# A two-layer graph network: part of layer 2's matrix products issued in layer 1, with one PSUM store for both layers

## The chip, the cores and the metric

The kernel runs on one core of one Trainium2 chip. The metric is the device time of the whole kernel in microseconds (us). Before the change it is 1557.31 us, the median of 9 runs (1549.85 to 1561.43).

A core has five engines that each run their own list of instructions in order: PE (matmuls; PEld are its weight loads), DVE (vector work), ACT (activations and copies), POOL (here: issuing gathers) and SP (here: issuing most transfers). They wait for each other by semaphores. ACT issues the writes of layer 1's result.

## The reference

```python
src, dst = edge_index                        # 100000 edges, sorted by dst; 6250 nodes
def _gin_agg(h, src, dst, eps, n_nodes):
    agg = jax.ops.segment_sum(h[src], dst, num_segments=n_nodes)
    return (1.0 + eps) * h + agg
h = _gin_agg(x, src, dst, eps1, n)           # x: 6250 x 256
h = jax.nn.relu(h @ W1a + b1a)               # 256 -> 512
h = jax.nn.relu(h @ W1b + b1b)               # 512 -> 512: the result h1 of layer 1
h = _gin_agg(h, src, dst, eps2, n)           # 512 wide
h = jax.nn.relu(h @ W2a + b2a)               # 512 -> 512
out = h @ W2b + b2b                          # 512 -> 256
x = _layernorm(x + out, axis=-1)
```

The destinations are drawn as 6250 u^2 with u uniform, so low nodes have many edges and high nodes few. All is float32.

## The kernel before

**Tiles.** Nodes stand in 49 tiles of 128 rows (the last has 106). Edges stand in 782 chunks of 128. Tiles 0 to 4 (`HEAVY`) are the heavy ones. Their edges, 240 chunks, are not gathered: layer 1 counts them into a table of how often each source appears for each heavy destination, and each layer multiplies this table with its input. The other 542 chunks are gathered, once in each layer.

**Gathered chunks.** `gather` (L255) issues one indirect transfer on POOL for each chunk, 128 rows of the layer's input: 128 KB in layer 1 and 256 KB in layer 2. Chunks go in pieces of four (`BURST`), and six pieces may be under way (`PIECES`), so 24 gathers. The seventh piece's first gather waits for the sums of the first piece. In layer 1 the pieces lie in `early`, in layer 2 in `early` and `late`. The sums (L992) are matmuls of a 0/1 selection (`sel`, made on DVE in `select`, L598) with the gathered rows; a group of such sums is copied by ACT (L1011, `split`), turned to its tile rows by one more matmul (L1023, with `to`, L603), called a union here, and added on DVE into the sums of each tile that it reaches (L1015, `acc`).

**Accumulators.** `seed` (L566) loads the layer's input for a block of two tiles (`TILES`) into a buffer `acc` (SP, L577; the last tile L583) and has ACT scale it by 1 + eps (L584). There are `ACCS` = 8 such buffers, and `held` lists the blocks that have one.

**Counting and products.** In layer 1 `counting` (L804) builds the table in `at`, an SBUF tile of 49 x 522 16-bit numbers per partition, and `convert` (L857) turns it part by part to float32, into `cf`, and writes it to `counts` in DRAM (SP, L860). A part is one heavy tile by one range of four tiles of sources (`RANGE`); there are 13 ranges and 5 heavy tiles, so 65 parts. `products` (L744) takes part by part: `xr` holds the range's input rows (SP, L757), `cf` the part of the table, and the product is 4 matmuls (L784; one for the last range). In layer 1 a heavy tile's 13 products share one sum in PSUM. In layer 2 the table is read back (L799), each product is a PSUM bank of 512 columns of its own, and DVE adds it into `acc` (L790). A turn's transfers are issued one turn ahead.

**Blocks.** When all edges of a block of two tiles are in, `block` (L678) transposes its sums (L704), multiplies by the first weights (L720) and the second (L734); `finish1` writes h1's rows (L1046, L1048, ACT's transfer L1049), `finish2` and `conclude2` add x, normalise and write the result (L1071 to L1088).

**Order.** All is written out by a planner in the kernel's Python. The main loop goes over the groups of gathered chunks; after each chunk it calls `tick`, which does what was put off by `later` (taking PSUM results waits `LAG` = 7 ticks), and lets two queues issue work: `blockwise` (blocks, two at a time) and `beside` (counting or products). `spread` sets the rate of `beside` so that PE's estimated work per chunk is level; the late chunks carry most of the blocks, so the products lie in the earlier ones. After the last chunk a loop drains both queues.

**The seam.** Layer 2's first gather may read any row of h1, so it waits until all are written. In layer 2, POOL first issues 24 gathers; PE's list begins with five products, and then the sums. Layer 2 has its own SBUF pools (`edge2`, `dense2`, with `xr` and `cf`) and its own PSUM pool, in the room that layer 1's pools leave.

Of the kernel before, what the change touches and what calls it, by code (L numbers as in the profile page):

```python
# [24 lines left out]
W = 10  # L25
# [4 lines left out]
AHEAD = 4  # L30
ACCS = 8
LAG = 7
# [107 lines left out]
def tile_gin_residual_layernorm(  # L140
# [354 lines left out]
    def rows(t):  # L495
        return min(P, N - t * P)
# [18 lines left out]
    def ordered(ctx):  # L515
# [17 lines left out]
        counts = odram.tile([len(ranges), HEAVY, P, RANGE * P], F32, name="counts")  # L533

        def layer(number, ctx, table, width, scale, wa, ba, wb, wide, prepare, finish, conclude):
            kk = width // P
            edge = ctx.enter_context(tc.tile_pool(name=f"edge{number}", bufs=3))
            dense = ctx.enter_context(tc.tile_pool(name=f"dense{number}", bufs=2))
            psum = ctx.enter_context(
                tc.tile_pool(name=f"psum{number}", bufs=1, space=bass.MemoryType.PSUM)  # L540
            )
            banks = [
                psum.tile([P, BANK], F32, tag=f"bank{i}", name=f"bank{i}") for i in range(BANKS)
            ]
            halves = [(i, j) for i in range(BANKS) for j in range(2)]
            acc = {}
            held = []
            places = [early]
            if number == 2:
                late = edge.tile([P, PIECES * BURST * D], F32, name="late", bufs=1)  # L550
                places.append(late)
            sels = {}
            once = number == 1
            left = {
                t: (0 if t >= HEAVY else 1 if once else len(ranges)) for t in range(NT)
            }
            uses = {t: 0 for t in range(NT)}
# [7 lines left out]

            def seed(ts):  # L566
                while len(held) >= ACCS:
                    if not blockwise.todo:
                        due(all=True)
                    assert blockwise.todo  # L570
                    blockwise.step()
                    tick()
                held.append(ts)
                a = edge.tile([P, TILES, width], F32, tag="acc", name="acc", bufs=ACCS)
                n = whole(ts)
                if n:
                    nc.sync.dma_start(  # L577
                        a[:, :n, :],
                        table[ts[0] * P : (ts[0] + n) * P, :].rearrange("(k p) d -> p k d", p=P),
                    )  # L580
                if n < len(ts):
                    nc.vector.memset(a[:, n, :], 0.0)
                    nc.sync.dma_start(a[: rows(ts[n]), n, :], table[ts[n] * P : N, :])  # L583
                later(5, lambda: nc.scalar.activation(  # L584
                    a[:, : len(ts), :], a[:, : len(ts), :], AF.Copy, scale=scale
                ))
                for i, t in enumerate(ts):
                    acc[t] = a[:, i, :]

            def select(g):  # L590
                c0, h = groups[g]
                n = min(PARTS * h, NCH - c0)
                small = h == 1
                sel = edge.tile(
                    [P, PARTS if small else GRP, SLOTS], F32, name="sel",
                    tag="sel1" if small else "sel", bufs=4 if small else 2,
                )
                nc.vector.tensor_tensor(  # L598
                    sel[:, :n, :], iota[:, :SLOTS].unsqueeze(1).to_broadcast([P, n, SLOTS]),
                    slot[:, c0 : c0 + n].unsqueeze(2).to_broadcast([P, n, SLOTS]), op=ALU.is_equal,  # L600
                )
                to = edge.tile([P, P], F32, tag="to", name="to", bufs=6)
                nc.vector.tensor_scalar(to, iota, home[:, g : g + 1], None, op0=ALU.is_equal)  # L603
                sels[g] = sel, to

            delayed = []
            now = 0

            def later(chunks, what, frees=False):
                delayed.append((now + chunks, what, frees))

            def undelay(item):
                delayed.remove(item)
                item[1]()

            def due(all=False):
                while delayed:
                    item = min(delayed, key=lambda d: d[0])  # L620
                    if not all and item[0] > now:
                        break
                    undelay(item)
                for b in list(waiting):
# [4 lines left out]
            def tick():  # L629
                nonlocal now  # L630
                now += 1
                due()

            opened = []

            def place(n, whole=False):

                while True:
                    here = [h for h in halves if h[0] not in opened]
                    single = [h for h in here if (h[0], 1 - h[1]) not in halves]
                    double = [h for h in here if (h[0], 1 - h[1]) in halves]
                    if 2 * n <= BANK and (single or double):
                        i, j = (single or double)[0]
                        mine = [(i, j)]
                        break
                    if 2 * n > BANK and double:

                        i = next(h[0] for k, h in enumerate(double) if (h[0], 1 - h[1]) in double[:k])
                        j = 0
                        mine = [(i, 0), (i, 1)]
                        break
                    undelay(min((d for d in delayed if d[2]), key=lambda d: d[0]))
                for h in mine:
                    halves.remove(h)
                if not whole:
                    opened.append(i)
                return banks[i][:, j * BANK // 2 : j * BANK // 2 + n], mine  # L660

            def complete(p):
                opened.remove(p[1][0][0])

            def free(p):
                halves.extend(p[1])

            def take_later(p, what):

                def take():  # L670
                    what(p[0])
                    free(p)

                later(LAG, take, frees=True)

            def block(ts):  # L678
# [20 lines left out]
                for i, t in enumerate(ts):  # L699
# [10 lines left out]
                    ))  # L710
                    if t == ts[-1]:
                        held.remove(ts)
# [31 lines left out]
            def products(turns, table_of):  # L744
# [28 lines left out]
                for i, (r, t) in enumerate(turns):  # L773
# [3 lines left out]
                    ks = ranges[r]  # L777
                    opens = not once or r == 0
                    closes = not once or r == len(ranges) - 1
                    if opens:  # L780
# [16 lines left out]

            def load_counts(cf, r, ks, t):
                nc.sync.dma_start(  # L799
                    cf[:, : len(ks), :].rearrange("p k j -> p (k j)"),  # L800
                    counts[r, t, :, : len(ks) * P],
                )

            def counting():  # L804

                assert HEAVY <= 2 * RING
                room = RING * P + W
                at = edge.tile([P, NT, room], mybir.dt.uint16, tag="at", name="at", bufs=1)  # L810
                F16 = mybir.dt.float16
# [139 lines left out]
            if number == 2:  # L951
                for i in range(PIECES):
                    gathered[i] = gather(i, table, width, *places)
            for b in blocks:
                if b[0] < HEAVY:
                    seed(b)
            due(all=True)
            select(order[0])
            select(order[1])
            blockwise = Queue(4.0, BLOCKS)  # L960
            work = 0.00167 * HEAVY * NT * width
            if number == 1:
                work += 8.0 + STEP * NC + ADD * len(STEPS)
                aside = counting()
            else:
                aside = products([(r, t) for r in range(len(ranges)) for t in heavy],
                                     load_counts)
            rates = spread(
                groups, N, E, PACES[number - 1] * work, 0.00167 * KH * (width + wide)
            )  # L970
            beside = Queue(rates[0])
            beside.todo.append(aside)
            if number == 2:
# [4 lines left out]
            for k, g in enumerate(order):  # L978
# [10 lines left out]
                while upto < len(pieces) and pieces[upto][0] == g:  # L989
# [11 lines left out]
                    for c, b in pieces[upto][1]:  # L1001
                        tick()
                        for q in both:
                            q.pump()
# [27 lines left out]
                if k + 2 < len(order):  # L1032
                    n = len(members[order[k + 1]])
                    later(n // 2 if n > PARTS else 0, lambda k=k: select(order[k + 2]))
            while any(q.todo for q in both) or waiting:
                for q in both:
                    q.step()
                    tick()
# [5 lines left out]
        def finish1(dense, t, m, po, i, early):  # L1044
# [3 lines left out]
            nc.scalar.activation(h[:m], y[:m], AF.Relu)  # L1048
            nc.scalar.dma_start(h1[t * P : t * P + m, :], h[:m])  # L1049

        def conclude1(dense, ts, early):
# [25 lines left out]
        def conclude2(dense, ts, early):  # L1077
# [17 lines left out]
            if n:  # L1095
# [3 lines left out]
                )  # L1099

        with ExitStack() as inner:
            layer(1, inner, x, D, e1[:, 0:1], w1a_s, b1a_s, w1b_s, H, prepare1, finish1, conclude1)
# [254 lines left out]
```

## Time and profile before

The profiled execution took 1555.25 us; the span of its records is 1553.5 us.

| What | us | Where from |
|---|---|---|
| median of 9 runs | 1557.31 | the times |
| the profiled execution, and the span in it | 1555.25, 1553.5 | the times |
| PE busy in the span | 1368.8 (88%) | page, part 1 |
| POOL busy in the span | 1044.8 (67%) | page, part 1 |
| DVE, ACT busy | 707.9 (46%), 390.8 (25%) | page, part 1 |
| 542 gathers of layer 1, mean of one | 0.973 | page, part 5 |
| L784, 980 records | 361.3 busy | page, part 5 |
| last gather of layer 1 starts | 701.29 | POOL in order of time |
| first and last gather of layer 2 start | 766.13, 1452.01 | POOL in order of time |
| last sum of layer 2 starts | 1472.36 | PE in order of time |

Layer 1 runs from about 40 to 766 and layer 2 from there to the end. A PE row counts records, of which a float32 matmul leaves two, so "x8" at L784 is one product. Their ends are modelled; the distance of the starts is the sounder number. Rows with "<-" name what ended the idle time before them. A granted clock (PEclk) of 1.00 is full speed.

### The profile page before, as it was taken

Reading aid. Unit: us, or ns where it says so; the run is one execution under the profiler, and the core shown is the slowest. Engines: PE = TensorE matmul, PEld = TensorE weight load, DVE = VectorE, ACT = ScalarE, POOL = GpSimd, SP = SyncE. Lnnn points to the kernel's source line nnn. Section 1 sums busy time; section 2 is a strip of 40 time slices with the busy share of each in tenths; the row PEclk is TensorE's granted clock in tenths of the full one; section 3 lists DMA queues with packets and bytes.
Section 4 is the critical chain, followed back from the end, with each engine's and each line's share of the span. In section 5 each row is a group of like instructions: output and inputs, shape, how many; then the busy total and the mean of one; then the engine's idle time right before and its main releaser. Section 6 shows DMA issues by size and latency. Waiting matters only on the chain.

```text
span 1553.5 us, 18728 instructions
## 1 busy us (share of the span) xinstructions
PE 1368.8 (88%) x6108; PEld 740.5 (48%) x6108; DVE 707.9 (46%) x2057; ACT 390.8 (25%) x831; POOL 1044.8 (67%) x1098
## 2 busy tenths in 40 slices
PE   2567887888999988999588899999999999999997
PEld 1134454554455445555322244444445555555576
DVE  6963455435556552233111223344444556465633
ACT  0433344323323232233210011111122222222222
POOL 6777777777777777770277777777777777677300
PEclk9778898889999999999888999999999999999999
DMA  6467686775657558741499888889888888778401
GB/s 186 148 215 239 186 267 189 226 227 161 185 184 227 156 169 271 230 136 61 157 315 306 275 255 293 297 291 317 247 289 284 285 283 278 232 235 258 138 27 42
DMA packets 165766, 340.57 MB, mean 219 GB/s; under 512 B 24628, under 2 KB 78110, under 8 KB 165660
## 3 DMA queue, kind: packets, MB, share of 16 engines
q0 software_dynamic: 69376, 213.19, 44.4%
q1 hardware_dynamic: 85776, 109.73, 21.2%
q10 hardware_dynamic: 10508, 16.35, 3.0%
q8 instruction: 52, 0.85, 0.2%
q14 instruction: 54, 0.44, 0.1%
HBM read 303.92 MB, written 35.26 MB: 218 GB/s over the span
## 4 chain that ended last, share of the span: by engine, by line
PE 67%; DMA 11%; POOL 9%; issue 6%; DVE 5%; ACT 1%; DVEq 0%; ACTq 0%; POOLq 0%; SPq 0%
PE bank L720 16%; PE bank L784 14%; PE bank L734 14%; PE bank L992 11%; PE bank L1023 9%; POOL early L255 7%; DMA early<-in_x_dram,srcs 5%; DMA late<-h,srcs 2%; POOL late L255 2%; DMA early<-h,srcs 2%; PE bank L704 2%; PE bank L869 2%; DMA xr<-in_x_dram 1%; DVE at L897 1%; DVE at L849 1%
## 5 line engine op out<-in xcount | busy, mean ns | idle before, releaser
L255 POOL DMA_INDIRECT early<-in_x_dram,srcs x542 | 527.4, 973 | 171.5 <-issue 147.2
L784 PE MATMUL bank<-xr,cf 128*128 128x256 f32 (+3 forms) x980 | 361.3, 514 | 22.0 <-issue 14.6
L255 POOL DMA_INDIRECT early<-h,srcs x276 | 262.8, 952 | 151.7 <-issue 72.5
L1015 DVE SCALAR_TENSOR_TENSOR acc<-bank,mask,acc 128x256 f32<-128x256 f32 (+1 forms) x430 | 241.9, 609 | 232.8 <-PE bank L1023 127.6
L255 POOL DMA_INDIRECT late<-h,srcs x266 | 252.0, 947 | 84.4 <-issue 67.0
L784 PEld LDWEIGHTS bank<-xr,cf 128*128 128x128 f32 (+1 forms) x980 | 194.0, 203 | 172.7 <-issue 144.8
L992 PE MATMUL bank<-early,sel 128*32 128x256 f32 (+1 forms) x1636 | 171.3, 494 | 71.7 <-DMA early<-in_x_dram,srcs 52.7
L720 PE MATMUL bank<-zt,w2a_s 128*128 128x256 f32 (+2 forms) x832 | 181.0, 371 | 4.7 <-DVE r L1071 4.7
L1023 PE MATMUL bank<-split,to 128*128 128x256 f32 (+1 forms) x372 | 176.4, 558 | 4.4 <-ACT zt L707 3.2
L734 PE MATMUL bank<-w1b_s,ht 128*128 128x512 f32 (+1 forms) x392 | 176.1, 594 | 0.4 <-ACT ht L724 0.4
L720 PEld LDWEIGHTS bank<-zt,w2a_s 128*128 128x128 f32 x832 | 151.6, 192 | 44.2 <-issue 18.4
L790 DVE TENSOR_TENSOR acc<-bank,acc 128x512 f32<-128x512 f32 (+1 forms) x70 | 46.9, 669 | 216.6 <-PE bank L784 198.0
L1011 ACT COPY split<-bank 128x256 f32<-128x256 f32 (+1 forms) x186 | 88.9, 481 | 220.0 <-PE bank L992 188.1
L833 DVE TENSOR_SCALAR ca<-numbers,low 128x128 f16<-128x128 f16 x240 | 65.3, 272 | 150.4 <-PE bank L869 150.4
L992 PEld LDWEIGHTS bank<-early,sel 128*32 128x32 f32 x1636 | 35.4, 112 | 174.6 <-issue 120.5
L1023 PEld LDWEIGHTS bank<-split,to 128*128 128x128 f32 x372 | 58.8, 197 | 122.2 <-issue 66.5
L734 PEld LDWEIGHTS bank<-w1b_s,ht 128*128 128x128 f32 (+1 forms) x392 | 73.0, 190 | 79.7 <-issue 71.0
L869 PE MATMUL bank<-cb,ca 128*128 128x490 f16 x240 | 86.2, 415 | 22.5 <-DVE cb L836 12.8
L720 PE MATMUL bank<-zt,w1a_s 128*128 128x256 f32 (+2 forms) x416 | 101.8, 385 | 1.9 <-ACT zt L707 1.1
L849 DVE TENSOR_TENSOR at<-cs,at 128x490 f16 x145 | 75.2, 519 | 49.0 <-ACT cf L857 30.6
L734 PE MATMUL bank<-w2b_s,ht 128*128 128x256 f32 (+1 forms) x392 | 91.7, 382 | 0.7 <-ACT ht L724 0.7
L720 PEld LDWEIGHTS bank<-zt,w1a_s 128*128 128x128 f32 x416 | 79.3, 201 | 20.7 <-issue 4.3
(115 smaller groups left out, 1005.2 us busy)
## 6 DMA issues: line engine op xcount, KB each, us to landing
xr<-in_x_dram SPq DMA_DIRECT2D x60, 512.0 KB, 4.6
counts<-cf SPq DMA_DIRECT2D x60, 256.0 KB, 4.5
cf<-counts SPq DMA_DIRECT2D x60, 256.0 KB, 6.9
h<-h1r ACTq DMA_DIRECT2D x48, 256.0 KB, 2.8
xr<-h SPq DMA_DIRECT2D x12, 1024.0 KB
acc<-h SPq DMA_DIRECT2D x23, 512.0 KB, 7.0
early<-in_x_dram,srcs POOLq DMA_INDIRECT x542
acc<-in_x_dram SPq DMA_DIRECT2D x23, 256.0 KB, 5.3
```

Of the source, the lines that this page charges most:

```text
L255: nc.gpsimd.indirect_dma_start(out=rows_[:, j, :], out_offset=None, in_=table, in_offset=bass.IndirectOffsetOnAxis(ap=srcs[:, c : c + 1], ...
L720: nc.tensor.matmul(ph[0][:, :nb], wa[:, k, f * P : (f + 1) * P], zt[:, k, :nb], start=(k == 0), stop=(k == kk - 1),)
L734: nc.tensor.matmul(po[0][:m], ht[:, f, i * P : i * P + m], wb[:, f, :], start=(f == 0), stop=(f == KH - 1),)
L784: nc.tensor.matmul(pm[0], cf[:m, j, :], xr[:m, j, :], start=(opens and j == 0), stop=(closes and j == len(ks) - 1),)
L790: nc.vector.tensor_tensor(acc[t], ap, acc[t], op=ALU.add)
L833: nc.vector.tensor_scalar(a, numbers[:, :P], low[:, c : c + 1], None, op0=ALU.is_equal)
L849: nc.vector.tensor_tensor(to, cs.rearrange("p (k w) -> p k w", w=W), to, op=ALU.add)
L869: mm = nc.tensor.matmul(pc[0], a, b, start=(i == 0), stop=(i == n - 1))
L992: mm = nc.tensor.matmul(pm[0][b * SLOTS : (b + 1) * SLOTS], sel[:, c - c0, :], rows_[:, j, :], start=(c == parts[b][0]), stop=(c == parts[ ...
L1011: nc.scalar.copy(split[:used], ap[:used])
L1015: nc.vector.scalar_tensor_tensor(acc[t], ap, mask[:, t - lo[g], g : g + 1], acc[t], op0=ALU.mult, op1=ALU.add,)
L1023: nc.tensor.matmul(pu[0], to[:used], split[:used], start=True, stop=True)
```

## The change

`products2`, a generator outside the layers, now issues layer 2's products. It takes a range as soon as all of its rows of h1 are written in the program (`written`), and may issue as many products as `allowed` says. In layer 1 it stands in `beside` behind `counting`; once that has ended, each gathered chunk allows 0.06 of a product (`BEGUN`). At the start of layer 2 the limit goes, and products are issued until each heavy tile's first has been taken from PSUM; then they go on in `beside`. Transfers are issued two turns ahead.

Its factors and sums lie in `at`, the room of the counts, which now lives through both layers: two buffers for a range of h1, four for parts of the table, five sums. The first product of a heavy tile is copied there by DVE and later ones are added. Layer 2's seeds of the heavy tiles are no longer scaled by ACT: DVE scales them and adds the sums. They don't count as held, and there are 6 accumulators instead of 8.

PSUM banks, their bookkeeping (`place`, `complete`, `free`, `take_later`) and the list of work put off are moved out of the layer, unchanged, so that both layers share them. `select` makes the selections of two small groups in one DVE operation each. `spread` gets only the work that is left. The loop at the end of each layer gives `blockwise` a step, and `beside` one only when that issued nothing; it no longer waits for `products2` in layer 1.

```diff
-ACCS = 8
+BEGUN = 0.06
+ACCS = 6
...
+        room = RING * P + W
+        shared = ctx.enter_context(tc.tile_pool(name="shared", bufs=1))
+        at = shared.tile([P, NT, room], mybir.dt.uint16, name="at")
+        written = set()
+        left2 = {t: (len(ranges) if t < HEAVY else 0) for t in range(NT)}
+        acc2 = {}
+        allowed = [0.0]
+        def products2():
+            flat = at.rearrange("p k j -> p (k j)").bitcast(F32)
...
+            xrs = [part(RANGE * H).rearrange("p (k d) -> p k d", d=H) for _ in range(2)]
+            cfs = [part(RANGE * P).rearrange("p (k j) -> p k j", j=P) for _ in range(4)]
+            sums = {t: part(H) for t in heavy}
...
+            def load():
+                if not turns:
+                    r = next((r for r in todo if written.issuperset(ranges[r])), None)
+                    if r is None:
+                        return
+                    todo.remove(r)
+                    turns.extend((r, t) for t in heavy)
+                    xr = xrs[n_ranges % 2]
...
+                        nc.sync.dma_start(
+                            xr[:, :whole, :],
+                            h1[ks[0] * P : (ks[0] + whole) * P, :].rearrange(
+                                "(k p) d -> p k d", p=P
+                            ),
+                        )
...
+                r, t = turns.pop(0)
+                cf = cfs[n_turns % 4]
+                nc.sync.dma_start(
+                    cf[:, : len(ranges[r]), :].rearrange("p k j -> p (k j)"),
+                    counts[r, t, :, : len(ranges[r]) * P],
+                )
+                loaded.append((r, t, xr, cf))
+            while todo or turns or loaded:
+                if len(loaded) < 2:
+                    load()
+                if not loaded or allowed[0] <= 0:
+                    yield None
+                    continue
+                allowed[0] -= 1
+                r, t, x_, cf = loaded.pop(0)
...
+                pm = place(H, whole=True)
+                for j, k in enumerate(ks):
+                    m = rows(k)
+                    nc.tensor.matmul(
+                        pm[0], cf[:m, j, :], x_[:m, j, :],
+                        start=(j == 0), stop=(j == len(ks) - 1),
+                    )
+                def add_product(ap, t=t):
+                    if t in acc2:
+                        nc.vector.tensor_tensor(acc2[t], ap, acc2[t], op=ALU.add)
+                    else:
+                        acc2[t] = sums[t]
+                        nc.vector.tensor_copy(acc2[t], ap)
+                    left2[t] -= 1
...
             def seed(ts):
+                ahead = number == 2 and ts[0] < HEAVY
...
-                held.append(ts)
+                if not ahead:
+                    held.append(ts)
...
-                later(5, lambda: nc.scalar.activation(
-                    a[:, : len(ts), :], a[:, : len(ts), :], AF.Copy, scale=scale
-                ))
...
+                    for i, t in enumerate(ts):
+                        nc.vector.scalar_tensor_tensor(
+                            acc[t], a[:, i, :], scale, acc[t], op0=ALU.mult, op1=ALU.add
+                        )
...
             def select(g):
+                if g in sels:
+                    return
                 c0, h = groups[g]
+                gs = [g]
+                if h == 1 and g + 1 < NG and len(members[g]) == PARTS:
+                    gs.append(g + 1)
...
+            blockwise = Queue(4.0, BLOCKS)
+            if number == 2:
+                allowed[0] = math.inf
+                while len(acc2) < HEAVY:
+                    next(ahead)
+                    tick()
...
+                work = PACES[1] * 0.00167 * sum(left2.values()) * RANGE * width
...
                     for c, b in pieces[upto][1]:
                         tick()
+                        if aside not in beside.todo:
+                            allowed[0] += BEGUN
...
-            while any(q.todo for q in both) or waiting:
-                for q in both:
-                    q.step()
+            while blockwise.todo or waiting or aside in beside.todo:
+                credit = blockwise.credit
+                blockwise.step()
+                tick()
+                if blockwise.credit == credit:
+                    beside.step()
                     tick()
...
             nc.scalar.dma_start(h1[t * P : t * P + m, :], h[:m])
+            written.add(t)
```

## The prediction

> **What bounds the kernel now.** I read the page's forty slices first, then the table of stages, then PE's and POOL's rows in order of time around three places: the end of layer 1, the seam between the layers, and the last moment at which PE waits for a gather.
>
> ```profile
> PE   2567887888999988999588899999999999999997
> POOL 6777777777777777770277777777777777677300
> core 0: us, PE busy (x) PEld busy (x) DVE busy (x) ACT busy (x) POOL busy (x), PEclk, DMA share, GB/s
> 600.00:700.00 100.00, 93.05 (x457) 54.73 (x456) 35.43 (x101) 30.20 (x74) 75.41 (x80) 0.98 0.66 208
> 766.00:822.00 56.00, 40.04 (x134) 14.41 (x138) 7.89 (x13) 4.50 (x5) 42.46 (x45) 0.80 0.95 329
> 822.00:900.00 78.00, 66.67 (x228) 22.05 (x228) 18.09 (x31) 5.25 (x8) 59.03 (x63) 0.89 0.88 291
> 900.00:1134.00 234.00, 233.69 (x961) 113.58 (x960) 86.53 (x185) 37.93 (x71) 177.12 (x187) 0.99 0.87 283
> 1300.00:1400.00 100.00, 98.97 (x441) 54.94 (x438) 58.01 (x135) 23.81 (x48) 70.95 (x76) 1.00 0.79 244
> 1453.00:1553.00 100.00, 87.26 (x446) 67.47 (x446) 38.95 (x100) 23.52 (x63) 0.09 (x1) 0.97 0.13 41
> ```
>
> POOL at seven tenths is full: one gather is busy 0.95 us and 0.30 us follow as issue, so 80 gathers fill 100 us. From 900 on PE is full too. Two engines share the bound, and the rows of single moments say which of them ends what.
>
> ```profile
> 683.30 7.03 PE L734 MATMUL bank<-w1b_s,ht 128*128 128x512 f32 x16
> 691.99 1.99 PE L720 MATMUL bank<-zt,w1a_s 128*128 128x256 f32 x8 [0.46 <-ACT zt L707]
> 753.61 3.68 PE L734 MATMUL bank<-w1b_s,ht 128*106 128x512 f32 x8 [0.43 <-ACT ht L724]
> 766.13 0.94 POOL L255 DMA_INDIRECT early<-h,srcs  x1 [63.89 <-DMA h<-h1r]
> 771.90 19.61 PE L784 MATMUL bank<-xr,cf 128*128 128x512 f32 x40 [14.61 <-issue]
> 791.44 2.78 PE L992 MATMUL bank<-early,sel 128*32 128x512 f32 x24
> 796.14 0.95 POOL L255 DMA_INDIRECT early<-h,srcs  x1 [0.30 <-issue]
> 808.66 4.51 PE L784 MATMUL bank<-xr,cf 128*128 128x512 f32 x8
> 904.55 3.43 PE bank L784 x8
> 1125.89 8.33 DMA late<-h,srcs
> 1134.35 1.06 PE L992 MATMUL bank<-late,sel 128*32 128x512 f32 x8 [0.67 <-DMA late<-h,srcs]
> 1452.01 1.08 POOL L255 DMA_INDIRECT late<-h,srcs  x1 [0.30 <-issue]
> ```
>
> Rows with one number less are pieces of the chain of waits (start, us). From about 650 to 757.3 (753.61 + 3.68) PE runs layer 1's dense work with gaps of 0.1 to 0.6 us only. The first gather of layer 2 (766.13) waits for the last row of h1. At 1134.35 PE waits for a gather for the last time; from there to the end, 419.2 us, it runs its list almost without a gap. The gather that it waits for there is the 288th of 542 ((1125.0 - 766.13) / 1.2505 = 287 before it). So the end is: the arrival of the 288th gather, plus all that stands behind it in PE's list.
>
> **The change, part by part.** What moves I read from the order in which the built programs issue each engine's instructions. One product of layer 2 is 4 matmuls of 128x512, 3.43 us (the row at 904.55).
>
> *Products.* Of 65, four now stand between layer 1's last sums, behind its last own product (about 650), and 13 instead of 5 stand in a row before layer 2's first sum. Behind the 288th gather's sum 14 are left instead of 21. The other work behind that point is the same in count (sums, unions, transposes, L720 and L734 matmuls). So PE's list from the last wait on is shorter by 7 x 3.43 = 24.0 us. This is the gain; the other five (12 - 7) are taken from the stretch 822 to 1134, where PE waits for gathers anyway, and are worth nothing.
>
> *Their price in layer 1.* 4 x 3.43 = 13.7 us in a stretch where PE has hardly a gap. The gaps seen there (0.16, 0.23, 0.46, 0.47, 0.56, 0.50, 0.43) are waits for ACT; some close when other work stands between. I take half of their 2.8 us back, less rounding: 12.4 us, by which h1's last row and all gathers of layer 2 begin later. Bounds: 10.9 (all gaps close) and 16.1 (none closes, and a seed comes 2.4 us late, which is the mean of ACT L584's nine waits for acc from x, 21.2 us in all).
>
> *Their price at the seam.* POOL may have 24 gathers ahead of PE (6 pieces of 4). Now PE reaches the first sums at 791.44, before the 25th gather (796.14), and POOL does not stop. After: PE ends layer 1 at 757.3 + 12.4 = 769.7. It need not wait 14.6 us for rows of h1, since two ranges of them and the tables of four products lie in the room of the counts by then, not in buffers that layer 1 still holds. 13 x 3.43 = 44.6 us bring it to 814.3, and the first piece of sums (1.06 us, as in the row at 1134.35) to 815.3. The 25th gather is due at 796.14 + 12.4 = 808.5. POOL stops 6.8 us. Bounds: 5.3 (layer 1 ends 1.5 us earlier for PE alone) and 20.8 (all 13 at the 4.51 us of the row at 808.66: 13 x 1.08 = 14.0 more). I take 6.8, the pace of 904.55: the row at 771.90 shows products near that pace while POOL gathers, 19.61 us for five, of which the first 4.4 us ran at half the clock (weight loads 0.86 us apart, then 0.43).
>
> *The clock there.* Those five cost 19.61 - 5 x 3.43 = 2.5 us more than at full clock, after an idle gap of 14.6 us; granted clock 0.80 in that stage. After the change the gap is gone, and I charge nothing. The Trainium skill ("TensorE: Matmul & The Clock Gate", Part 1, the HAM clock gate) says that the array is throttled to half after an idle window of about 3.4 us, and stays there for about 3.4 us of work; by the page alone the gap at 757 to 772 would have cost an estimated 1.7 us, where the row says 2.5. Read against the change, it says that longer waits for gathers after 815 would cool PE again, each at that price.
>
> A product after a wait for gathers is slow as well: the row at 808.66, 4.51 - 3.43 = 1.1 us. Such losses lie where the gathers decide; without that cover each costs 1.1 us.
>
> *SP's queue.* The first two loads of h1 (1 MB each) and ten of tables (256 KB) now stand ahead of layer 1's last three seeds and layer 2's first. The fifth table needs a buffer that the first moved product frees (about 654); the last seed was issued at 681. 27 us of cover; without it the last block is late by the load's 5.3 us. The same bytes are moved in all.
>
> *Accumulators 8 to 6, heavy ones held apart.* Some seeds stand a few transfers later in SP's list of layer 1, PE's order is the same: nothing, up to the 2.4 us in the bound above. In layer 2 three ACT scalings (2.8 us at 759) become five operations on DVE (609 ns mean of L1015: 3 us), and DVE is a third busy: nothing.
>
> *Selections in pairs.* 372 DVE operations become 248. DVE is 35% busy in the 600s; PE waits for it at L992 3.7 us in the whole run. Between 0 and -3.7; I take 0. *One PSUM store:* the wait at 771.90 was for loads, so 0. *The last loop* changes which block stands where in the tail, not how much: one of PE's 0.52 us waits for DVE r goes, -0.5.
>
> **Sum.** -24.0 + 12.4 + 6.8 - 0.5 = -5.3. The profiled span of 1553.5 becomes 1548.2. The profiled execution took 1555.25 (1.75 outside the span) and the median is 1557.31, 2.06 above it: 1548.2 + 1.75 + 2.06 = 1552.0 us.
>
> **Rivals.** All on the median's scale. A measurement of this kernel can tell about 0.3% (4.7 us) from no change.
>
> *Layer 1 hides its four products.* Then 12.4 goes: 1539.6. For it: PE is 93% busy in the 600s, so 7 us per 100 are free. Against: those gaps close before 650, and behind it there are 2.8 us. 13%.
>
> *POOL's pace decides to the last gather.* Then the 24.0 is not to be had: the 19.2 us by which POOL is late, less the 9.2 us that it waits now (1453.1 - 766.13 - 542 x 1.2505), less 10.3 us of PE work that no longer stand behind the last sum (12 matmuls of L720 and 8 of L734 at 0.43, 8 transposes at 0.21): -0.3, 1557.0. For it: POOL is full through 1300. Against: in 1300 to 1400 POOL is at 70.95 instead of 75.6, so it waits for PE there. 20%.
>
> *The seam stalls* (the case on the other side). The 13 products in a row want 460 KB each (table, and a fifth of 1 MB), while gathers take 256 KB per 1.25 us and DMA is 95% busy in that stage: 460 / 3.43 + 256 / 1.25 = 339 GB/s are wanted, 329 were moved from 766 to 822. If the products run at 4.51 us, POOL stops 20.8 us instead of 6.8: +8.7, 1566. It decides from 5.3 / 13 = 0.41 us more per product. For it: a table's load waits for the product four before it, so it has 3 x 3.43 = 10.3 us to land, and takes 6.9 us in the median now. Against: four products find their factors loaded, and DMA is only 19% busy from 700 to 766. 22%.
>
> **How the numbers follow.** The forecast has 45%: its own range is 1546 to 1558 (below: -1.5, -1.5 and DVE's -3.7; above: +3.7 in layer 1 and 2.5 of cold clock at the seam), of which 27 points lie below 1552.6 and 18 within. Hidden products: 13, all faster. POOL's pace: 5 faster, 12 within, 3 slower. The stalled seam: 2 within, 20 slower. Faster 0.45, same 0.32, slower 0.23. The range takes in the two outer cases: 1539 to 1566.
>
> **What would show it.** Right: L1's last h1 row 11 to 15 us later; 13 products from about 770 without a gap in front; one stop of POOL of 5 to 10 us near the 25th gather of layer 2; more PE waits for gathers up to 1100; the last such wait near the 288th gather, with 14 products behind it. Wrong: layer 1 ending where it did (then the first rival); POOL stopping over 12 us (the third); PE waiting for gathers beyond 1300 (the second). A wait of the first products for rows of h1 would break the working at the seam.

## The result, and the profile after

The changed kernel takes 1567.65 us (median of 10 runs, 1564.87 to 1573.23) against 1555.83 for the kernel before (31 runs): a ratio of 1.0079, 95% interval 1.0065 to 1.0094. It is slower, and lies just outside the range that was given. The profiled execution's span is 1565.0 us against 1553.5, so 11.5 us have to be found.

First the forty slices of the page, then the table of stages of the changed kernel, with the columns of the table before.

```profile
PE   2567787788998988899996889999999999999897
POOL 6777777777777777671066777777777777777600
```

```profile
600.00:700.00 100.00, 90.65 (x405) 53.25 (x402) 29.00 (x68) 26.37 (x63) 70.61 (x75) 0.93 0.69 223
766.00:822.00 56.00, 54.81 (x152) 25.83 (x151) 15.02 (x24) 4.32 (x12) 23.56 (x24) 1.00 0.69 247
822.00:900.00 78.00, 57.42 (x218) 17.46 (x217) 14.38 (x26) 7.42 (x9) 56.03 (x59) 0.82 0.85 269
900.00:1134.00 234.00, 221.99 (x912) 106.74 (x911) 80.18 (x168) 35.68 (x66) 177.35 (x187) 0.97 0.86 283
1300.00:1400.00 100.00, 97.36 (x482) 57.38 (x481) 61.09 (x128) 27.46 (x57) 75.83 (x80) 1.00 0.82 254
1453.00:1553.00 100.00, 94.04 (x471) 69.37 (x470) 43.56 (x106) 23.77 (x58) 20.15 (x20) 0.98 0.31 94
```

PE is now full at the seam (54.81 of 56 us where it was 40.04), but in the 600s it is busy 90.65 instead of 93.05 although it was given work there, and from 900 to 1134 it idles 12 us where it idled 0.3. POOL still gathers after 1453, where it was done before. So the seam is filled as intended; layer 1 ended later than the work put into it explains, and all gathers of layer 2 with it. The rows of single moments (ACT, SP's queue, PE, POOL, in order of time) show where.

```profile
644.95 0.30 ACT L964 CAST cf<-at 128x128 f32<-128x128 uint16 x1 [0.40 <-ACT h1r L1166]
645.69 0.78 SPq L651 DMA_DIRECT2D at<-h  x1
646.52 1.00 SPq L662 DMA_DIRECT2D at<-counts  x2
657.13 5.46 PE L682 MATMUL bank<-at 128*128 128x512 f32 x8 [4.86 <-DMA at<-counts]
678.42 3.60 PE L682 MATMUL bank<-at 128*128 128x512 f32 x8
775.74 3.68 PE L853 MATMUL bank<-w1b_s,ht 128*106 128x512 f32 x8 [0.43 <-ACT ht L843]
779.25 27.63 PE L682 MATMUL bank<-at 128*128 128x512 f32 x64
789.21 0.94 POOL L256 DMA_INDIRECT early<-h,srcs  x1 [76.45 <-DMA at<-counts]
826.29 0.94 POOL L256 DMA_INDIRECT early<-h,srcs  x1 [6.52 <-PE bank L1105]
1159.39 1.93 PE L1105 MATMUL bank<-late,sel 128*32 128x512 f32 x8 [3.12 <-issue]
1468.51 2.66 PE L839 MATMUL bank<-zt,w2a_s 128*128 128x256 f32 x8 [3.73 <-ACT zt L826]
1471.10 1.94 PE L1105 MATMUL bank<-late,sel 128*32 128x512 f32 x8
```

In this order: the last conversion of the counts (644.95) frees their room, and the first loads of the moved products go out at 645.69. The first product needs one of them at 652; it waits 4.86 us and then runs at a lower clock (granted clock 0.66 from 657.13 to 662.43), 5.46 us where the next takes 3.60. Layer 1's last matmul ends at 779.42 (before: 757.29), and the first gather of layer 2 goes at 789.21 (766.13). The 13 products at the seam run at 3.45 us each (27.63 / 8), without a gap in front. POOL stops once, 6.52 us. The last wait for a gather is at 1159.39 (before 1134.35; the row says issue, but in the chain of waits the gather's transfer stands in front of it, from 1150.93), and a new wait stands at 1468.51, behind ACT.

From that last wait to the end it is 405.6 us (before 419.15). So 25.0 us were lost up to it and 13.5 gained behind it, which are the 11.5.

Beside the first three experiments the kernel before took 1556.58 us and beside all later ones 1786 to 1805, with idle stretches of PE for which the traces name no releaser in the program, so the later ones are read by their ratios and against each other only.

### The profile page after: what moved, and what is told of

The parts are those of the page before. It is cut to its first block, busy times and chain, and to the rows that moved or that the text cites. A ratio compares the mean times of both kernels' runs of the same rounds, so it can differ in the third digit from the quotient of the medians.

```text
span 1565.0 us, 18566 instructions
## 1 busy us (share of the span) xinstructions
PE 1362.8 (87%) x6108; PEld 738.5 (47%) x6108; DVE 702.6 (45%) x1938; ACT 388.4 (25%) x828; POOL 1051.7 (67%) x1098
## 3 DMA queue, kind: packets, MB, share of 16 engines
q1 hardware_dynamic: 85776, 109.73, 20.8%
## 4 chain that ended last, share of the span: by engine, by line
PE 54%; DMA 15%; POOL 14%; issue 9%; DVE 5%; ACT 1%; DVEq 0%; ACTq 0%; SPq 0%; POOLq 0%
PE bank L839 13%; PE bank L853 13%; POOL early L256 11%; PE bank L1105 8%; PE bank L682 7%; PE bank L1138 7%; DMA early<-in_x_dram,srcs 6%; POOL late L256 3%; DMA late<-h,srcs 3%; PE bank L902 3%; DMA early<-h,srcs 2%; DMA at<-counts 2%; PE bank L823 1%; PE bank L976 1%; DVE at L1004 1%
## 5 line engine op out<-in xcount | busy, mean ns | idle before, releaser
L256 POOL DMA_INDIRECT late<-h,srcs x266 | 255.4, 960 | 81.0 <-issue 67.3
L682 PE MATMUL bank<-at 128*128 128x512 f32 (+1 forms) x490 | 230.1, 616 | 7.6 <-DMA at<-counts 7.6
L839 PE MATMUL bank<-zt,w2a_s 128*128 128x256 f32 (+2 forms) x832 | 179.0, 369 | 7.3 <-ACT zt L826 5.2
L839 PEld LDWEIGHTS bank<-zt,w2a_s 128*128 128x128 f32 x832 | 150.6, 191 | 44.6 <-issue 17.5
L682 PEld LDWEIGHTS bank<-at 128*128 128x128 f32 (+1 forms) x490 | 94.4, 198 | 131.3 <-issue 124.8
L902 PE MATMUL bank<-xr,cf 128*128 128x256 f32 (+1 forms) x490 | 127.1, 405 | 5.4 <-DMA xr<-in_x_dram 4.0
L689 DVE TENSOR_TENSOR at<-bank,at 128x512 f32<-128x512 f32 x60 | 41.3, 689 | 180.3 <-PE bank L682 180.3
L902 PEld LDWEIGHTS bank<-xr,cf 128*128 128x128 f32 (+1 forms) x490 | 99.3, 206 | 29.2 <-issue 9.3
L839 PE MATMUL bank<-zt,w1a_s 128*128 128x256 f32 (+2 forms) x416 | 103.7, 390 | 1.9 <-ACT zt L826 1.1
L976 PE MATMUL bank<-cb,ca 128*128 128x490 f16 x240 | 82.8, 400 | 24.6 <-DVE cb L943 12.4
```

Source lines behind the costliest of these rows:

```text
L256: nc.gpsimd.indirect_dma_start(out=rows_[:, j, :], out_offset=None, in_=table, in_offset=bass.IndirectOffsetOnAxis(ap=srcs[:, c : c + 1], ...
L682: nc.tensor.matmul(pm[0], cf[:m, j, :], x_[:m, j, :], start=(j == 0), stop=(j == len(ks) - 1),)
L839: nc.tensor.matmul(ph[0][:, :nb], wa[:, k, f * P : (f + 1) * P], zt[:, k, :nb], start=(k == 0), stop=(k == kk - 1),)
L902: nc.tensor.matmul(pm[0], cf[:m, j, :], xr[:m, j, :], start=(opens and j == 0), stop=(closes and j == len(ks) - 1),)
L976: mm = nc.tensor.matmul(pc[0], a, b, start=(i == 0), stop=(i == n - 1))
```

## The experiments

**No product in layer 1.**

```diff
-BEGUN = 0.06
+BEGUN = 0.0
-                for _ in range(6):
+                for _ in range(2):
```

> No product runs in layer 1 (the allowance grows by 0 a chunk and the fixed steps after the seam fall from 6 to 2); the seam keeps its 13 products and 9 stay behind the 288th gather of layer 2, as in the changed kernel. Theory A: the four products are the whole lateness of layer 1, none hidden, 10.3 us for the first (4.86 of wait for its table and 5.46 of matmuls) and 3.6 for each other, 21.1 in all. Then the first gather of layer 2 goes at 768 instead of 789.2 and the time is 1567.7 - 21.1 = 1546.6, below the kernel before. Rival B: the six blocks of running sums in place of eight, the paired selections or the new closing loop make layer 1 late, and the products lie in time that PE had: the first gather stays behind 780 and the time stays above 1560.

Measured: 1551.73 us, 0.9968 of the kernel before (interval 0.9948 to 0.9987), so 15.9 below the changed kernel and, by a little, faster than the kernel before. Its profiled execution was above that median (span 1555.0). In order of time on PE and POOL:

```profile
757.75 3.68 PE L853 MATMUL bank<-w1b_s,ht 128*106 128x512 f32 x8 [0.43 <-ACT ht L843]
806.99 5.37 PE L682 MATMUL bank<-at 128*128 128x512 f32 x8 [3.97 <-DMA at<-counts]
812.28 2.78 PE L1105 MATMUL bank<-early,sel 128*32 128x512 f32 x24
771.70 0.95 POOL L256 DMA_INDIRECT early<-h,srcs  x1 [64.52 <-DMA at<-counts]
813.65 0.95 POOL L256 DMA_INDIRECT early<-h,srcs  x1 [12.25 <-PE bank L1105]
```

Layer 1 ends at 761.43 instead of 779.42, and the first gather goes 17.5 us earlier; the six blocks, the paired selections and the new loop are all still in place, so Theory B falls. It is 5 us short of Theory A. At the first gather 17.5 of its 21.1 are there. In the profiled execution 5.0 of them are lost again up to the last wait for a gather, where the seam got worse: a product waits 3.97 us for its table and is slow after it, and POOL stops 12.25 us instead of 6.52. Another 2.5 are lost behind that wait. What the products cost in layer 1 is best read from where layer 1's own last product starts (the row of two matmuls, 649.41 before and 651.68, 654.18, 652.22 after) to its last matmul's end:

| us | before | changed | none in layer 1 | first one later |
|---|---|---|---|---|
| layer 1's own last product starts | 649.41 | 651.68 | 654.18 | 652.22 |
| layer 1's last matmul ends | 757.29 | 779.42 | 761.43 | 772.34 |
| between them | 107.9 | 127.7 | 107.2 | 120.1 |
| first gather of layer 2 | 766.13 | 789.21 | 771.70 | 782.11 |
| last wait of PE for a gather | 1134.35 | 1159.39 | 1146.84 | 1152.74 |
| span | 1553.5 | 1565.0 | 1555.0 | 1560.5 |

Without the products the stretch is as long as before (107.2 and 107.9); with them it is 19.9 us longer than before. (The run with products earlier in layer 2, below, has the changed kernel's layer 1, and there the stretch is 127.5.) The first line of the table shows a smaller loss that the products can't have made, as none has run by then: in the traces of the changed program, with 651.61 in the run below, this moment lies 2.2 to 4.8 us later than before. What makes it late was not taken apart.

**The first product later.**

```diff
-        allowed = [0.0]
+        allowed = [-0.6]
```

> The allowance starts at -0.6 instead of 0, so the first of the four products in layer 1 comes some ten chunks after its loads were issued; four stay in layer 1, 13 in the seam and 9 behind the 288th gather. Theory A: the 4.86 us of wait for the table and the 1.9 that the eight matmuls after it took beyond 3.6 go, the first gather of layer 2 goes at about 782.4 and the time is 1567.7 - 6.8 = 1560.9. Rival B: what ends layer 1 is another chain and the wait is hidden, the time stays within 2 of 1567.7.

Measured: 1561.21 us, ratio 1.0032 (1.0012 to 1.0051); 6.4 us below the changed kernel, as Theory A had it. The four products in the profile (PE, in order of time):

```profile
664.42 3.60 PE L682 MATMUL bank<-at 128*128 128x512 f32 x8
685.43 3.60 PE L682 MATMUL bank<-at 128*128 128x512 f32 x8
706.42 3.60 PE L682 MATMUL bank<-at 128*128 128x512 f32 x8
725.40 3.60 PE L682 MATMUL bank<-at 128*128 128x512 f32 x8
```

No wait for a table and no slow product is left, and the stretch of the table is 120.1 us: the wait for the first product's table, with the slow matmuls after it, was worth 7.6, and four products that come in time cost 120.1 - 107.9 = 12.2 (12.9 against the run without them).

**Products earlier in layer 2.**

```diff
-PACES = (1.1, 1.08)
+PACES = (1.1, 1.5)
```

> The pace of layer 2's products is 1.5 instead of 1.08: all are done before the 288th gather (9 stood behind it), 4 fewer stand behind the 92nd chunk. Theory A: up to about 925 PE waits 27 us for gathers, so products pulled there cost nothing, and those pulled into the full stretch from 930 to 1134 only change places: 4 x 3.43 = 13.7 gained at most, time about 1555. Rival B: the sums slip behind the products, gathers come later with them and what is gained behind the 288th gather is lost before it: 1567.7 within 3. Rival C: with the products gone from the end, the pairs of the last blocks stand alone and PE waits for ACT and DVE more often: slower than 1570.

Measured: 1555.69 us, ratio 1.0003 (0.9988 to 1.0018): 12.0 us below the changed kernel, from one number. The table of stages and a row of PE from this run:

```profile
822.00:900.00 78.00, 64.39 (x244) 21.04 (x243) 16.72 (x29) 7.52 (x9) 55.78 (x59) 0.91 0.86 278
1000.00:1134.00 134.00, 134.00 (x547) 64.27 (x546) 54.33 (x118) 22.00 (x42) 101.40 (x108) 1.00 0.88 295
914.92 1.07 PE L1105 MATMUL bank<-late,sel 128*32 128x512 f32 x8 [0.23 <-issue]
1376.91 5.59 PE L839 MATMUL bank<-zt,w2a_s 128*128 128x256 f32 x16 [5.50 <-ACT zt L826]
```

From 822 to 900 PE does 64.39 us of work instead of 57.42, and no wait for a gather is left after 914.92 (the changed kernel's last is at 1159.39). Theory B falls. Theory C is there in part: with no products left in the tail PE waits more for ACT (from layer 2's first gather on, 8.8 us at L839 for `zt` against 5.2), the longest 5.50 at 1376.91, but that takes only a part of the gain.

**Nine at the seam instead of 13.**

```diff
-                for _ in range(6):
+                for _ in range(2):
```

> Two fixed steps after the seam instead of six: 4 products in layer 1 as changed, 9 instead of 13 at the seam, the four that leave it stand among the first 92 chunks of layer 2, and from there on TensorE's order is that of the changed kernel (9 behind the 288th gather). Theory A: the first sum of layer 2 goes 4 x 3.43 = 13.7 us earlier, before POOL has filled its 24 buffers, so POOL's stop of 6.52 us goes, every later gather and the wait near 1159 come 6.5 earlier, and the four products fall into waits that PE has up to 925 anyway (27 us): 1567.7 - 6.5 = 1561.2. Rival B: the transfers, and not POOL, set the pace of the gathered rows there, the stop lies beside their backlog and nothing is gained: 1567.7 within 2.5.

> As e5_seam_nine, on a chip on which the kernel before takes about 1556. Theory A: the first sum of layer 2 goes 4 x 3.43 = 13.7 us earlier, POOL's stop of 6.52 us goes, the wait near 1159 comes 6.5 earlier, and the four products fall into PE's waits up to 925: 1567.7 - 6.5 = 1561.2. Rival B: the transfers set the pace of the gathered rows there and the stop lies beside their backlog: 1567.7 within 2.5. The ratio to the kernel before in e5_seam_nine, 1.0077, is that of the changed kernel and speaks for B, but there each engine stood in places that the trace here doesn't show.

> Nine products at the seam instead of 13, else the changed kernel. Theory A, POOL's stop of 6.52 us is on the path: 6.5 below the changed kernel of the same call. Rival B, the rows come at the transfers' pace and the stop lies beside it: within 2.5 of the changed kernel, as the ratios 1.0077 and 1.0059 of the two runs so far against 1.0079 suggest.

> Nine products at the seam, else the changed kernel. Theory A (POOL's stop of 6.52 is on the path): 1561.2 where the kernel before takes 1556, ratio 1.0034; on the last chip the trace had the stop at 3.89 instead of 14.40 and the median 10.4 lower. Rival B (the stop lies beside the transfers): ratio 1.007 to 1.009.

Measured against the kernel before: 1.0077 (1.0037 to 1.0117), 1.0059 (1.0032 to 1.0085), 1.0071 (1.0039 to 1.0102), 1.0036 (1.0013 to 1.0060). Beside the third of these runs stood the changed kernel itself:

> The changed kernel itself, on the chip of the three other runs of this call. Where the kernel before takes about 1556: 1567.7, ratio 1.0079. Where it takes some 1790: theory A (the loss is the four products in layer 1, matmuls and a wait for a table, and not a property of one chip) ratio 1.006 to 1.011; rival B (on a chip where every engine waits more, the moved products fall into waits) ratio below 1.004.

It took 1805.13 us, ratio 1.0106 (1.0049 to 1.0162), so the loss is there at this pace too. It ran on the chip of the first experiments; the changed kernel itself has no run that is known to be from another. There POOL's stop is, in the changed kernel and then in the one with nine:

```profile
950.24 0.94 POOL L256 DMA_INDIRECT early<-h,srcs  x1 [14.40 <-PE bank L1105]
```

```profile
935.78 0.95 POOL L256 DMA_INDIRECT early<-h,srcs  x1 [3.89 <-PE bank L1105]
```

The stop is 10.5 us shorter and the median 10.4 lower (1794.77), as Theory A wants it. But against the kernel with seven blocks below, which keeps 13 products at the seam and stops 15.5 to 17.1 us where the one with nine stops 3.5 to 4.4, the same kernel was 2.1 us slower once and 1.4 and 6.3 faster in two other pairs. What the stop is worth, between nothing and its length, is left open.

**Seven blocks of sums.**

```diff
-ACCS = 6
+ACCS = 7
```

> Seven blocks of running sums in place of six and nothing else (TensorE's products stand as in the changed kernel: 4, 13, and 9 behind the 288th gather). Theory A: the load of the last block, which waited for a free block until 1457.6, goes earlier, ACT doesn't stand before it, and the wait for zt of 3.73 and the slow matmuls behind it (0.85 and 0.87) go: 1567.7 - 5.4 = 1562.3. Rival B: another wait takes its place (PE waits for zt in the run without products in layer 1 too): 1567.7 within 2.

> As e6_seven_sums, on a chip on which the kernel before takes about 1556. Theory A: the load of the last block goes earlier than 1457.6, and the wait for zt of 3.73 and the slow matmuls behind it go: 1567.7 - 5.4 = 1562.3. Rival B: another wait takes its place: 1567.7 within 2.

> Seven blocks of running sums, else the changed kernel. Theory A: the load of the last block goes well before 1457, no wait of PE for zt of over 1 us near it, 5.4 less: 1562.3, ratio 1.0041. Rival B: another wait takes its place, ratio 1.007 to 1.009.

Eight blocks were to be the first trial, but with `at` kept through both layers they don't fit: layer 2's `dense2` needs 20.3 KB per partition, and 18.1 are left. So there is no result for eight.

Measured for seven: 1.0077 (1.0031 to 1.0123), 1.0075 (1.0057 to 1.0094), 1.0062 (1.0039 to 1.0084): not to be told from the changed kernel's 1.0079. The theory that the last block's load waits for a free block holds for a small part only: that load is issued 106 to 110 us before the end of the span in these three runs, 107 in the changed kernel (1565.0 - 1457.63) and 105 in its second trace, and SP's order in layer 2 is the same with seven. With six, SP stands 1.5 us at that load for a free block (6.3 in the second trace). With seven that wait is gone, and the load goes hardly earlier, behind the transfer that stands before it in SP's list. So most of the wait at 1468.51 has another reason. ACT's row, before and then changed:

```profile
1452.28 0.72 ACT L584 ACTIVATE acc<-acc,e 128x512 f32<-128x512 f32 x1 [8.93 <-DVE r L1072]
1452.91 1.05 ACT L1011 COPY split<-bank 128x512 f32<-128x512 f32 x2
```

```profile
1466.78 0.72 ACT L745 ACTIVATE acc<-acc,e 128x512 f32<-128x512 f32 x1 [9.88 <-DVE r L1190]
1467.41 1.05 ACT L826 COPY zt<-bank 128x512 f32<-128x512 f32 x2
```

In both kernels ACT stands some 9 us before the scaling of the last block. In the changed kernel the row names DVE, but the chain of waits names what ends the wait, the landing of that block's own load (start, us):

```profile
1457.63 9.06 DMA acc<-h
```

In the three runs with seven blocks, and in the second trace of the changed kernel, the row itself names the load. In the kernel before, the trace doesn't tell whether it was the load. What is queued behind it differs: before, a copy of `split`, and PE lost 1.24 us; now the copies of `zt` that PE's next L839 matmuls wait for, and PE loses 3.73 and then clock. In the four later traces with the same order PE loses between nothing and 3.44 us there. Which part of the change places them there was not tried; with seven blocks they stand there too. An earlier load of this block was not tried either.

**The kernel before, with its products earlier.**

```diff
-PACES = (1.1, 1.08)
+PACES = (1.1, 1.5)
```

> The kernel before, with the pace of layer 2's products at 1.5 instead of 1.08: 4 more of them stand before the 92nd chunk, and 3 instead of 16 behind the 288th gather. Theory A: what pays is that products stand where PE waits for gathers, and this needs nothing of the change: the waits from 801 to 897 (19.8 us) take four products, 13.7 us at most, 12 as in the run of the changed kernel at this pace: 1556 - 12 = 1544. Rival B: here PE is full from 900 to 1134, so 9 of the 13 products delay sums there, the 288th gather's sum slips and nothing is gained: 1556 within 3.

> As e7_before_pace_1.5, on a chip on which the kernel before takes about 1556. Theory A: the waits from 801 to 897 (19.8 us) take four products more: 1556 - 12 = 1544. Rival B: the products pulled into the full stretch from 900 to 1134 delay the 288th gather's sum and nothing is gained: 1556 within 3.

> The kernel before with the pace of layer 2's products at 1.5. Theory A, the products that fill PE's waits for gathers pay without any of the change: 12 below the kernel before, ratio 0.992 (two runs so far: 0.9927 and 0.9876). Rival B, nothing is gained where the kernel before takes about 1556, as its PE is full from 900 to 1134: ratio 0.998 to 1.002.

> The kernel before with the pace of layer 2's products at 1.5. Theory A, products in PE's waits for gathers pay without the change: 1544, ratio 0.992 (three runs so far: 0.9927, 0.9876, 0.9891). Rival B, PE is full from 900 on where the kernel before takes 1556, so they only change places: ratio 0.998 to 1.002.

Measured: 0.9927 (0.9904 to 0.9950), 0.9876 (0.9848 to 0.9905), 0.9891 (0.9835 to 0.9947), 0.9874 (0.9843 to 0.9905). Theory A: one number in the old kernel gives 0.7 to 1.3%, with nothing of the change. No run of it stands beside a kernel before of 1556 us, so the gain there is not shown.

**All parts together.** No product in layer 1, no fixed steps after the seam, so 11 products there, pace 1.5 and seven blocks:

```diff
-PACES = (1.1, 1.08)
+PACES = (1.1, 1.5)
-BEGUN = 0.06
-ACCS = 6
+BEGUN = 0.0
+ACCS = 7
-                for _ in range(6):
+                for _ in range(0):
```

> None of the products in layer 1, 11 at the seam, a pace of 1.5 in layer 2, seven blocks of running sums. Theory A, the parts add up: 1551.7 (no products in layer 1) - 12 (pace) - 6.9 (two products fewer before the first sum, of POOL's stop of 12.25) - 5.4 (blocks) = 1527. Rival B: pace, seam and blocks fill or remove the same waits of PE, so that only the larger counts: about 1540. Rival C: with no products left behind the 288th gather, the last pairs wait for ACT and DVE, which takes back more than half of it: 1545 or more.

> As e8_all_parts, on a chip on which the kernel before takes about 1556. Theory A, the parts add up: 1551.7 - 12 (pace) - 6.9 (two products fewer before the first sum) - 5.4 (blocks) = 1527. Rival B: pace, seam and blocks fill or remove the same waits of PE: about 1540. Rival C: with no products left behind the 288th gather the last pairs wait for ACT and DVE: 1545 or more.

> No product in layer 1, 11 at the seam, pace 1.5, seven blocks of running sums. Theory A, parts add: about 0.981 of the kernel before (1527 of 1556). Rival B, they fill the same waits of PE: 0.988 to 0.993 (two runs so far: 0.9903 and 0.9907), no better than the kernel before with the pace alone.

Measured: 0.9903 (0.9865 to 0.9942), 0.9907 (0.9871 to 0.9943), 0.9929 (0.9904 to 0.9955). Faster than the kernel before, and than the changed kernel where that ran beside it (1773.25 against 1805.13), but the parts don't add up to the 0.981 of Theory A. The ratios are Rival B's; that the parts fill the same waits was not looked up in the traces. Against the kernel before at the same pace it is level in two pairs (1770.38 and 1769.19, and 1787.57 and 1783.89, which lie within the spread of the single times) and 5.8 us slower in one (1773.25 and 1767.41). With the pace raised, no gain from the rest of the change is left to be seen here.

## Why the prediction was wrong

The bound was read rightly: the end is the arrival of a gather near the 288th plus PE's list behind it. Its sum was -24.0 + 12.4 + 6.8 - 0.5 = -5.3; the profile says +11.5.

*"Their price in layer 1", 12.4: this is the term that failed. Measured: 23.1* (766.13 to 789.21). The four products themselves cost 12.2, close to the predicted figure. What was missing is the load in front of the first, 7.6 (the run with the first product later shows it): a wait that the sum put at nothing. The working under "SP's queue" looked at the fifth table, which has 27 us of cover, and at the last seed, but not at the first: its room comes free only with the last conversion at about 645, and the planner lets the first product go one chunk later, since the allowance is above zero after one chunk. The diff shows both. A 256 KB table took 6.9 us in the median in the trace of before, so one issued at 646.52 lands at 653.4, behind the 652.3 at which PE asks. That there is a wait could be worked out, but only 1.1 us of it: here PE could start 10.6 us after the issue. Of the rest, 2.3 lay before layer 1's own last product and 1.0 between its last matmul and the first gather; neither was taken apart. 12.2 + 7.6 + 2.3 + 1.0 = 23.1.

*"Their price at the seam", 6.8: right in the trace,* 6.52, by the mechanism named (13 products at full pace, one stop of POOL at the 25th gather). What it costs in time stays open.

*The 24.0 behind the 288th gather: right in its products, short by some 6 in what came of them.* PE's last wait is now for the piece that ends with the 284th gather (POOL's rows, counted from 789.21, have it at 1152.31), one piece of four earlier, so one piece of sums and one product more, 1.06 + 3.43 = 4.5 us, stand behind it. It comes 25.0 later: 23.1, POOL's stop of 6.2 beyond the usual 0.30, less 5.0 for four gathers, and 0.7 that remain (up to that gather POOL's other gathers took 2.1 longer, and from its issue to PE's sum it was 1.4 less). From there to the end 24.0 - 4.5 = 19.5 us less PE work should give -19.5; measured are -13.5. PE's busy time fell by 16.3 us (403.1 to 386.9), 3.2 less than that, and its idle time rose by 2.7. The 3.2 match a lower clock after the waits at 1159.39 and 1468.51: the four rows behind them took some 3.4 us more than the same work elsewhere, at a granted clock of 0.50 to 0.85. The step that failed here is that the tail's order "changes which block stands where in the tail, not how much": which block stands behind ACT's late scaling decided 2.5 us of waiting (3.73 against 1.24) and about 1.6 of clock behind it. That the last loop makes this order, and not another part of the change, is not shown.

*The rivals.* "Layer 1 hides its four products" fell (12.2 of 13.7 show). "The seam stalls" had nearly the measured time, 1566, and the wrong mechanism: the products ran at 3.45 us, not 4.51, and POOL stopped 6.52, not 20.8. "POOL's pace decides to the last gather" fell too, though POOL is now full through 1400 (75.83 of 100): PE's last wait for a gather is at 1159.39. The sign to look for, "layer 1's last h1 row 11 to 15 us later", was the one that told at first sight that the sum was off: the row came 22 us later.

*What a product is worth where it stands.* The prediction gave the five products taken out of 822 to 1134 no worth. The other direction was not asked: products moved *into* that stretch. The pace of 1.5 did that and gained 12.0 us, more than the whole change was forecast to; and the kernel before gains by it too, 0.7 to 1.3% in the four runs above. (The experiments' expectations count nine products behind the 288th gather where the prediction has 14: they leave out the five of the last range, of one matmul each.)

## What to carry to other kernels

Work moved to an earlier stage starts where its inputs land, not where the code first allows it: for the first moved step take the moment at which its buffer comes free, add a load's time from the trace, and compare that with the moment at which the engine asks for it. Before moving work across stages, look whether its own stage has waits of the same engine that it could fill: here one pace constant did more than the rebuilt seam. A wait that stands unseen before an off-path engine (ACT's 9 us) gets a price as soon as an edit changes what is queued behind it.

## What the runs showed of the hardware

The Trainium skill ("TensorE: Matmul & The Clock Gate", Part 1, the HAM clock gate) has PE at half clock after an idle window of about 3.4 us. The first fence is from the changed kernel, the second from the run without products in layer 1, rows of PE in order of time:

```profile
1049.88 1.94 PE L1105 MATMUL bank<-early,sel 128*32 128x512 f32 x8 [2.79 <-issue]
```

```profile
852.61 1.93 PE L1105 MATMUL bank<-early,sel 128*32 128x512 f32 x8 [2.93 <-issue]
868.35 1.06 PE L1105 MATMUL bank<-late,sel 128*32 128x512 f32 x8 [2.83 <-DMA late<-h,srcs]
```

Gaps of 2.79, 2.93 and (at 1159.39) 3.12 us were followed by sums at 1.93 or 1.94 us instead of 1.06, at a granted clock of 0.50; one of 2.83 was not, at 1.00. So shorter gaps than the page's figure can cost the clock, and the length of a gap alone does not decide it.
